# Graph attention setup: one product of 80 condition columns for neighbours and condition rows, weights loaded by chunk, and one self product moved in the loop

## The chip, the cores and the metric

The kernel runs on one core of a Trainium2 chip. The metric is the device time of one launch in microseconds (us); lower is better. A core has a matrix engine (TensorE, PE in the profile, with PEld for its weight loads), a vector engine (VectorE, DVE), a scalar engine (ScalarE, ACT), a general one (GpSimd, POOL), and SyncE (SP), which here only issues loads and stores (DMAs). ACT issues some loads too. The engines run side by side, each through its own list of instructions in order, and wait for one another on semaphores.

## The reference

Two blocks follow each other: a graph attention block over x (4 batches of 1024 rows of 512), and a transformer block modulated by a condition (4 rows of 512). All is float32. The part that the change touches is the graph block:

```python
def _forward(v, q, adj, W_self, b_self, w_bias, b_bias, Wq, bq, Wk, bk, Wout, bout):
    row_zero = v.sum(-1) == 0
    q_exp = jnp.where(row_zero[..., None], 0.0, q[:, None, :])
    vcq = jnp.concatenate([v, q_exp], axis=-1)
    self_feat = vcq @ W_self.T + b_self
    output = self_feat
    for d in range(2):
        A = adj_f if d == 0 else jnp.swapaxes(adj_f, 1, 2)
        A = A[:, :, :20, :]
        cond, vb = A.sum(-1), A @ w_bias + b_bias
        output = output + _gat_attention(self_feat, cond, vb, Wq[d], bq[d], Wk[d], bk[d], Wout[d], bout[d])
    return v + relu(output)

def _gat_attention(self_feat, cond_adj, label_bias, Wq, bq, Wk, bk, Wout, bout):
    kv = self_feat[:, :20]                       # the first 20 rows of a batch are the neighbours
    qh = (self_feat @ Wq.T + bq)                 # 16 heads of 32
    kh = (kv @ Wk.T + bk)
    aff = einsum('bnhd,bmhd->bnhm', qh, kh) / sqrt(32)
    aff = where(cond_adj[:, :, None, :] > 0, aff, -9e15) + label_bias[:, :, None, :]
    w = softmax(aff, axis=-1)
    out_t = einsum('bnhm,bmf->bnhf', w, kv)
    return einsum('bnhf,hgf->bnhg', out_t, Wout) + bout
```

The condition q enters the self features of a row only where the row's sum is not zero. So self_feat is x @ Wx + nonzero * (q @ Wq_in) + b_self, where Wx and Wq_in are the two halves of W_self, transposed. Behind it come layer norms, attention with 16 heads of 64 and a hidden layer of 2048, all modulated by the silu of the condition times W_mod. The change touches of these only the silu.

## The kernel before

The order of every engine's instructions is that in which the program is written (a manual schedule); tiles are freed by semaphores. A load carries one of eight completion semaphores in turn, and waits until the load eight places before it in the program has landed, no matter which queue either is on.

*Setup (L186 to L389).* It prepares what the graph loop reads, for 80 neighbours (4 batches of 20).

- Loads. ACT's queue issues the 80 neighbour rows into vcq (L193, four loads, one for each batch), the four condition rows cnd (L196), and the condition spread over 20 rows for each batch into the right half of vcq (L198, four loads). SP's queue issues wx (L195) and wq_in (L201), one megabyte each, then five small loads of bias vectors into rows (L210), then six weights of one megabyte (L216: for each direction d the key, output and query weights) and the output bias (L217), then the first three tiles of x, masks and small constants.
- Warming (L240): seven products of a zero tile into the banks that the loop uses first.
- neighbours(0) (L250 to L254) transposes the 80 rows with four TensorE transposes and copies them to vcqT; through_self(0) (L256 to L267) multiplies them with wx: 16 matmuls of 128x128 weights and 80 columns. DVE meanwhile finds the rows whose sum is not zero (nz, L244 and L245) and multiplies the spread condition with it (L270). neighbours(1) and through_self(1) do the same with the spread condition and wq_in, into the same bank pf.
- Between them: silu of the condition on ACT (L274), and transposes of the condition and of its silu (L279, L280). Then the vectors are transposed (L283) and the bias is added (sfT, L286).
- The condition rows' own product with wq_in (L293: four condition columns as weights, 512 columns streamed, four matmuls) gives qrows; it is stored and read back spread over 128 partitions as qrB (L298 to L300).
- keys(d) (L307), values(d) (L331), and folded(d) (L366) make keys, values and folded query weights from sfT; ACT and DVE take turns to evacuate. Between them g_sum and g_start of tiles 0 and 1 stand in ACT's and DVE's lists.

*The graph loop (L861 and on)* runs over 32 tiles of 128 rows, with its stages spread over steps s. What belongs here, by helper and line:

- g_start(i) (L182, L183, DVE): the nonzero flag of each row, then flag times qrB plus b_self, written straight into the bank pf. g_self(i) (L666, PE) adds x @ wx on it, in four matmuls of 512 columns; g_selfout (L674, ACT) copies it to sf; g_selfT (L679, PE and L681, ACT) transposes it.
- g_mask1(i) (L686, L688, POOL) makes floats of the mask (af) and multiplies them by the label weights (ab); af and ab have one buffer each. g_mask2(i) (L695 to L699, DVE) sums both to a factor and a term for each neighbour.
- g_scores (L706, PE), g_soft1 (L719, DVE), g_soft2 (L729, POOL), g_soft3 (L736, L737, DVE: maximum and subtraction), g_soft4 (L740, ACT: exp), g_soft5 (L745, L746, DVE: sum and reciprocal; L748, POOL: weights), g_weightsT (L755, PE; L756, ACT), g_startattend (L761, ACT), g_attend (L767, PE), g_rows (L779, DVE). g_startscores (L662, ACT) presets the bank of the scores.

The order of one step s before the change is:

```python
            do(g_scores, s)
            do(g_weightsT, s - 1)
            do(g_soft1, s)
            do(g_startscores, s + 1)
            do(g_startattend, s - 1)
            do(g_soft2, s)
            do(g_mask2, s + 2)
            do(g_mask1, s + 3)
            do(g_soft3, s)
            do(g_self, s + 2)
            do(g_selfT, s + 1)
            do(g_soft4, s)
            do(g_soft5, s)
            do(g_attend, s - 1)
```

and then g_selfout(s + 2), g_rows(s - 1), g_start(s + 3), g_sum(s + 4). The bank pa of the scores, the tile t of the softmax and the tile wts exist once each, so the softmax of one tile ends before that of the next begins.

Of the kernel before, what the change touches and what calls it, by code (L numbers as in the profile page):

```python
# [26 lines left out]
GH, GD, NG, NL = 16, 32, 20, 11  # L27
# [14 lines left out]
def cond_block_kernel(  # L42
# [27 lines left out]
    nc = tc.nc  # L70
    B = cond.shape[0]
    NTA = B * NT
    KV = B * NG
# [5 lines left out]
    def evac(k, o, i):  # L79

        if k % 2 == 0:
            nc.scalar.copy(o, i)
        else:
            nc.vector.tensor_copy(o, i)
# [4 lines left out]
    ident = cst.tile([P, P], F32, name="ident")  # L89
# [6 lines left out]
    V_SELF, V_K, V_Q, V_1, V_MOD = 0, FC, 3 * FC, 5 * FC, 5 * FC + MC  # L96
    vecs = cst.tile([P, N_VEC], F32, name="vecs")
# [34 lines left out]
    with ExitStack() as gctx:  # L132
# [8 lines left out]
        wx = gp.tile([P, FC, F], F32, name="wx")  # L141
        scT = gp.tile([P, FC, 32], F32, name="scT")
# [22 lines left out]
        nzs, pfs, pas, pos = {}, {}, {}, {}  # L165
# [19 lines left out]
        with ExitStack() as sctx:  # L185
            sp = sctx.enter_context(tc.tile_pool(name="sp", bufs=1))  # L186
            sps = sctx.enter_context(tc.tile_pool(name="sps", bufs=3, space=PSUM))


            vcq = sp.tile([KV, 2 * F], F32, name="vcq")  # L190
            cnd = sp.tile([B, F], F32, name="cnd")
            for b in range(B):
                nc.scalar.dma_start(vcq[b * NG : (b + 1) * NG, :F], x[b * S : b * S + NG, :])  # L193
            wq_in = sp.tile([P, FC, F], F32, name="wq_in")
            nc.sync.dma_start(wx, w_selfT[:F].rearrange("(c p) f -> p c f", p=P))  # L195
            nc.scalar.dma_start(cnd, cond)  # L196
            for b in range(B):
                nc.scalar.dma_start(  # L198
                    vcq[b * NG : (b + 1) * NG, F:], cond[b : b + 1, :].broadcast_to([NG, F])
                )  # L200
            nc.sync.dma_start(wq_in, w_selfT[F:].rearrange("(c p) f -> p c f", p=P))  # L201
            rows = sp.tile([N_VEC, P], F32, name="rows")
            for at, v in (
                (V_SELF, b_self.rearrange("(c p) -> c p", p=P)),
                (V_K, gbk.rearrange("d (c p) -> (d c) p", p=P)),
                (V_Q, gbq.rearrange("d (c p) -> (d c) p", p=P)),
                (V_1, b1.rearrange("(c p) -> c p", p=P)),
                (V_MOD, b_mod.rearrange("(c p) -> c p", p=P)),
            ):
                nc.sync.dma_start(rows[at : at + v.shape[0], :], v)  # L210
# [25 lines left out]
            for i in range(2):  # L236
                pfs[i] = bank_of("pf", i)
            pas[0], pos[0] = bank_of("pa", 0), bank_of("po", 0)
            for t in (pfs[0], pfs[1], pas[0][:, 0, :], pas[0][:, 1, :], pos[0], pos[0], pos[0]):
                nc.tensor.matmul(t, lhsT=warm[:, :P], rhs=warm, start=True, stop=True)  # L240


            nz = sp.tile([KV, 1], F32, name="nz")
            nc.vector.tensor_reduce(nz, vcq[:, :F], axis=AX.X, op=ALU.add)  # L244
            nc.vector.tensor_scalar(nz, nz, 0.0, None, ALU.not_equal)  # L245
            vcqT = sp.tile([P, 2 * FC, KV], F32, name="vcqT")
            pf = sps.tile([P, FC, KV], F32, name="pf", tag="s")

            def neighbours(h):
                pt = sps.tile([P, FC, P], F32, name="pt", tag="s")  # L250
                for c in range(FC):
                    k = h * FC + c
                    nc.tensor.transpose(pt[:, c, :KV], vcq[:, k * P : (k + 1) * P], ident[:KV, :KV])
                evac(h, vcqT[:, h * FC : (h + 1) * FC, :], pt[:, :, :KV])  # L254

            def through_self(h):  # L256
                w = (wx, wq_in)[h]
                for c in range(FC):
                    for k in range(FC):
                        nc.tensor.matmul(  # L260
                            pf[:, c, :],
                            lhsT=w[:, k, c * P : (c + 1) * P],
                            rhs=vcqT[:, h * FC + k, :],
                            start=(h == 0 and c == 0 and k == 0),
                            stop=(h == 1 and k == FC - 1),
                            skip_group_check=True,
                        )  # L267

            neighbours(0)
            nc.vector.tensor_scalar(vcq[:, F:], vcq[:, F:], nz, None, ALU.mult)  # L270
            through_self(0)
            neighbours(1)
            silu = sp.tile([B, F], F32, name="silu")
            nc.scalar.activation(silu, cnd, AF.Silu)  # L274
            condT = sp.tile([P, FC, B], F32, name="condT")
            for t, src in ((condT, cnd), (scT[:, :, :B], silu)):
                pc = sps.tile([P, FC, B], F32, name="pc", tag="s")
                for c in range(FC):
                    nc.tensor.transpose(pc[:, c, :], src[:, c * P : (c + 1) * P], ident[:B, :B])  # L279
                nc.vector.tensor_copy(t, pc)  # L280
            through_self(1)
            pv = sps.tile([P, F], F32, name="pv", tag="s")
            nc.tensor.transpose(pv[:, :N_VEC], rows, ident[:N_VEC, :N_VEC])  # L283
            nc.vector.tensor_copy(vecs, pv[:, :N_VEC])
            sfT = sp.tile([P, FC, KV], F32, name="sfT")
            nc.vector.tensor_tensor(  # L286
                sfT, pf, vecs[:, V_SELF : V_SELF + FC].unsqueeze(2).to_broadcast([P, FC, KV]), ALU.add
            )


            pq = sps.tile([P, F], F32, name="pq", tag="s")
            for c in range(FC):
                nc.tensor.matmul(  # L293
                    pq[:B], lhsT=condT[:, c, :], rhs=wq_in[:, c, :], start=(c == 0), stop=(c == FC - 1)
                )
            qrows = sp.tile([B, F], F32, name="qrows")
            nc.scalar.copy(qrows, pq[:B])
            nc.sync.dma_start(qrd, qrows)  # L298
            for b in range(B):
                nc.sync.dma_start(qrB[:, b, :], qrd[b : b + 1, :].broadcast_to([P, F]))  # L300
# [543 lines left out]
        def do(f, i):  # L844
            if 0 <= i < NTA:
                f(i)
# [14 lines left out]
        for s in range(-4, NTA + 2):  # L861
            do(g_load, s + 4)
            if s >= -2:
                do(g_loadmask, s + 4)
            if s in (1, 7, 13, 23):
                g_modload(s // 6)
            do(g_scores, s)
            if s == NTA:
                ahead(4)
            do(g_weightsT, s - 1)  # L870
            do(g_soft1, s)
            do(g_startscores, s + 1)
# [51 lines left out]
    with ExitStack() as actx:  # L924
# [298 lines left out]
        for b in range(B):  # L1223
# [22 lines left out]
            for gp in range(NP):  # L1246
                g, p = divmod(gp, 2)
                at = s0 + gp * NT
# [80 lines left out]
        for i in range(4):  # L1329
            at = NS - (10, 9, 6, 3)[i]  # L1330
# [149 lines left out]
        for s in range(NS + 1):  # L1480
# [4 lines left out]
            if s < NS:  # L1485
                b, r = divmod(s, NP * NT)
                gp, t = divmod(r, NT)
# [218 lines left out]
```

## Time and profile before

| | us |
|---|---|
| median of 3 runs | 3044.85 |
| lowest and highest | 3044.52, 3045.57 |
| the profiled execution | 3043.88 |
| its span, first to last instruction | 3041.9 |

The span falls into stretches like this (busy time of an engine in each):

| stretch, us | what runs | PE | DVE | ACT | POOL |
|---|---|---|---|---|---|
| 0 to 22.9 | setup up to keys(0) | 20.58 | 3.46 | 3.62 | 5.06 |
| 22.9 to 59.4 | keys, values, folded weights | 36.30 | 14.41 | 11.95 | 1.59 |
| 59.4 to 100 | first steps of the graph loop | 36.66 | 22.92 | 14.00 | 15.58 |
| 100 to 405 | rest of the graph loop | 300.27 | 251.55 | 129.37 | 129.73 |
| 405 to 3041 | attention, output, hidden layer | 2610.37 | 1704.51 | 1272.01 | 1186.35 |

How to read the lines of the profile: the timeline gives start, length, engine, line of the code, operation, what is written from what, shapes and count, and in brackets the idle time of the engine just before and what ended it. The chain of waits is followed back from the last instruction of a window, and gives start, length and what, in order of time. SPq and ACTq are the issue of loads by these engines. A float32 matmul stands in the trace as two instructions of TensorE; a transpose as one. A busy time of PE counts pipelined matmuls and is not a measure of full use.

### The profile page before, as it was taken

The numbers are of one execution on the slowest core, as the hardware profiler recorded it, in microseconds if no ns is written. First come the engines' busy times: TensorE is split into PE (matmuls) and PEld (weight loads), VectorE is DVE, ScalarE is ACT, GpSimd is POOL, SyncE is SP. The second block draws the span as 40 slices with busy tenths as digits, with TensorE's granted clock in tenths as the row PEclk, the third lists the DMA queues.
The fourth block names the chain that finished last, engine by engine and source line by source line (L and its number), as shares of the span: only waits on it lengthen the run. The fifth ranks groups of instructions, "written<-read, shape, count | busy, mean of one in ns | idle before, by whom it ended". The sixth has DMA issues, their size and how long they took to land.

```text
span 3041.9 us, 41802 instructions
## 1 busy us (share of the span) xinstructions
PE 3004.2 (99%) x15327; PEld 1977.4 (65%) x15327; DVE 1996.9 (66%) x2833; ACT 1430.9 (47%) x2367; POOL 1338.3 (44%) x922
## 2 busy tenths in 40 slices
PE   9999999999999999999999999999999999999999
PEld 5666655555555555555555555555568888888888
DVE  3788867787878887878877878877863222222322
ACT  2444456555755555755555755555641221122211
POOL 1444456555655655656655656655721110111010
PEclk9999999999999999999999999999999999999999
DMA  6433447777868767868767867776871010101110
GB/s 195 133 124 107 139 111 189 167 160 177 196 156 207 190 158 173 199 160 204 189 162 166 204 164 197 189 168 152 213 190 69 14 49 28 49 18 38 35 42 15
DMA packets 282719, 418.06 MB, mean 137 GB/s; under 512 B 28912, under 2 KB 101036, under 8 KB 282516
## 3 DMA queue, kind: packets, MB, share of 16 engines
q1 hardware_dynamic: 282268, 415.06, 53.6%
q8 instruction: 123, 2.02, 0.3%
q14 instruction: 80, 0.66, 0.1%
q10 hardware_dynamic: 248, 0.34, 0.0%
HBM read 121.09 MB, written 25.76 MB: 48 GB/s over the span
## 4 chain that ended last, share of the span: by engine, by line
PE 81%; DVE 7%; ACT 4%; issue 3%; POOL 2%; DMA 2%; SPq 1%; POOLq 0%; DVEq 0%; ACTq 0%
PE q L520 18%; PE psc L1139 14%; PE pav L1047 13%; PE mbd L520 5%; PE pu L1122 5%; PE mbu L520 5%; PE mad L520 4%; PE mau L520 3%; ACT w L1156 2%; PE mcd L520 2%; PE mdd L520 2%; DVE mx L1150 2%; PE mdu L520 2%; PE mcu L520 2%; POOL t L729 1%
## 5 line engine op out<-in xcount | busy, mean ns | idle before, releaser
L1165 POOL TENSOR_SCALAR w<-w,sm 128x1024 f32<-128x1024 f32 x256 | 727.8, 2843 | 704.4 <-DVE sm L1161 700.2
L1156 ACT ACTIVATE w<-psc,mx 128x1024 f32<-128x1024 f32 x512 | 570.1, 1114 | 642.1 <-DVE mx L1150 641.0
L1174 DVE STREAM_TRANSPOSE wd<-w 128x1024 f32<-128x1024 f32 x512 | 632.0, 1235 | 109.0 <-ACT w L1163 97.5
L1150 DVE TENSOR_REDUCE mx<-psc 128x1 f32<-128x1024 f32 x512 | 599.0, 1210 | 80.4 <-PE psc L1139 77.2
L1139 PE MATMUL psc<-kT,qT 64*128 64x512 f32 x2048 | 528.2, 615 | 3.8 <-ACT w L1156 1.5
L1047 PE MATMUL pav<-wT,v 128*64 128x256 f32 x4096 | 480.0, 383 | 1.8 <-DMA wT<-wd 1.8
L1047 PEld LDWEIGHTS pav<-wT,v 128*64 128x64 f32 x4096 | 292.0, 137 | 226.7 <-issue 84.5
L1139 PEld LDWEIGHTS psc<-kT,qT 64*128 64x128 f32 x2048 | 200.7, 186 | 223.3 <-issue 151.3
L1163 ACT ACTIVATE w<-w,sm 128x1024 f32<-128x1024 f32 x256 | 291.0, 1137 | 0.0
L499 POOL TENSOR_TENSOR tx<-hT 128x512 f32<-128x512 f32 x8 | 10.3, 1288 | 596.7 <-ACT hT L435 596.7
L1131 DVE TENSOR_TENSOR xr<-pu,xr 128x512 f32<-128x512 f32 x210 | 143.4, 683 | 79.5 <-PE pu L1122 79.3
L520 PE MATMUL q<-hT,wqk 128*128 128x512 f32 (+1 forms) x396 | 181.2, 581 | 1.0 <-DVE q L534 1.0
L542 ACT COPY mbu<-mau 128x512 f32<-128x512 f32 x30 | 17.1, 570 | 276.6 <-PE mau L520 276.6
L706 PE MATMUL pa<-kp,sfT 128*128 128x320 f32 x512 | 143.5, 433 | 1.5 <-ACT sfT L681 1.5
L520 PEld LDWEIGHTS q<-hT,wqk 128*128 128x128 f32 x396 | 74.7, 190 | 80.9 <-issue 78.3
L520 PE MATMUL q<-tx,ex 128*128 128x512 f32 (+1 forms) x264 | 123.5, 591 | 1.4 <-ACT hT L435 1.4
L706 PEld LDWEIGHTS pa<-kp,sfT 128*128 128x128 f32 x512 | 94.8, 190 | 38.2 <-ACT sfT L681 1.9
L666 PE MATMUL pf<-wx,xT 128*128 128x512 f32 x256 | 117.0, 601 | 0.0
L520 PE MATMUL mad<-w,hs 128*128 128x256 f32 x512 | 113.1, 379 | 0.0
L520 PEld LDWEIGHTS mad<-w,hs 128*128 128x128 f32 x512 | 97.3, 190 | 13.2
L1122 PE MATMUL pu<-wout,oT 128*128 128x256 f32 x360 | 98.4, 396 | 4.2 <-DVE sm L1161 2.2
L1122 PEld LDWEIGHTS pu<-wout,oT 128*128 128x128 f32 x360 | 62.6, 189 | 59.2 <-issue 31.6
(303 smaller groups left out, 4592.8 us busy)
## 6 DMA issues: line engine op xcount, KB each, us to landing
wT<-wd SPq DMA_DIRECT2D x1024, 256.0 KB
wqk<-in_w_qkv SPq DMA_DIRECT2D x64, 256.0 KB
xT<-in_xt SPq DMA_DIRECT2D x32, 256.0 KB
xs<-in_x SPq DMA_DIRECT2D x32, 256.0 KB
x1d<-xs SPq DMA_DIRECT2D x32, 256.0 KB
xl<-x1d SPq DMA_DIRECT2D x32, 256.0 KB
wv<-in_w_qkv SPq DMA_DIRECT2D x32, 256.0 KB
xr<-x1d SPq DMA_DIRECT2D x32, 256.0 KB
```

Of the source, the lines that this page charges most:

```text
L520: nc.tensor.matmul(t[:, q * width : (q + 1) * width], lhsT=lhs(which, q, k), rhs=rhs(which, q, k), start=(fresh and q == 0 and k == 0), st ...
L666: nc.tensor.matmul(pfs[i], lhsT=xT[i][:, c, :], rhs=wx[:, c, :], start=False, stop=(c == FC - 1), skip_group_check=True,)
L706: nc.tensor.matmul(pas[i][:, n, :HF], lhsT=sfT2[i][:, c, :], rhs=kp[:, b, c, n * HF : (n + 1) * HF], start=False, stop=(c == FC - 1), skip ...
L1047: nc.tensor.matmul(po[j * D : (j + 1) * D, :], lhsT=vt[b, g][:, m, p * P + j * D : p * P + (j + 1) * D], rhs=w[:, j, :, m, :], start=(m == 0),
L1122: nc.tensor.matmul(pu[0][:, q * HB : (q + 1) * HB], lhsT=a[:, q * P : (q + 1) * P], rhs=r, start=(bool(fresh) and q == 0), stop=True, skip ...
L1131: nc.vector.tensor_tensor(o, pu[0].rearrange("p (r f) -> p r f", r=2), o, ALU.add)
L1139: nc.tensor.matmul(sc[j][:, n * F : (n + 1) * F], lhsT=qT[b, gp][q, t * P : (t + 1) * P], rhs=kT[b, gp][q, n * F : (n + 1) * F], start=Tru ...
L1150: nc.vector.tensor_reduce(mx, sc, axis=AX.X, op=ALU.max, negate=True)
L1156: nc.scalar.activation(w, sc, AF.Exp, bias=mx, accum_out=sm)
L1163: nc.scalar.mul(w, w, sm)
L1165: nc.gpsimd.tensor_scalar(w, w, sm, None, ALU.mult)
L1174: nc.vector.transpose(wd[j][:, :, at, :], wn.pop((b, gp, t, j)).rearrange("p (m k) -> p m k", k=U))
```

## The change

- wq_in and wx are loaded in four chunks of 128 rows each, wq_in first. The spread condition is no longer loaded (vcq is half as wide). cnd is issued first on ACT's queue, and the five loads of rows move from SP's queue to ACT's, behind the neighbours.
- The warming does five products and not seven.
- The condition is transposed first (condT), spread on DVE to 80 columns (condB), and multiplied with wq_in once (pq). The result is copied to cq. Its first column for each batch (qT_) gives the condition rows, by four transposes (pr) instead of the product of 512 columns.
- The flag nz is brought into columns by a small product with the identity (pn, nzB), and multiplies cq after the product, on DVE. The bias is then added, and last the neighbours' product with wx (pf).
- through_self runs over the chunks k outside and over the output blocks c inside.
- The silu of the condition and its transposes come after the neighbours' product.
- In the loop, g_self(3) stands in step 1 directly behind the scores, ahead of the transposes of the weights. In step 0, g_start(3) and g_mask2(2) change places.

```diff
-            vcq = sp.tile([KV, 2 * F], F32, name="vcq")
+            vcq = sp.tile([KV, F], F32, name="vcq")
             cnd = sp.tile([B, F], F32, name="cnd")
-            for b in range(B):
-                nc.scalar.dma_start(vcq[b * NG : (b + 1) * NG, :F], x[b * S : b * S + NG, :])
             wq_in = sp.tile([P, FC, F], F32, name="wq_in")
-            nc.sync.dma_start(wx, w_selfT[:F].rearrange("(c p) f -> p c f", p=P))
             nc.scalar.dma_start(cnd, cond)
             for b in range(B):
-                nc.scalar.dma_start(
-                    vcq[b * NG : (b + 1) * NG, F:], cond[b : b + 1, :].broadcast_to([NG, F])
-                )
-            nc.sync.dma_start(wq_in, w_selfT[F:].rearrange("(c p) f -> p c f", p=P))
+                nc.scalar.dma_start(vcq[b * NG : (b + 1) * NG, :], x[b * S : b * S + NG, :])
+            for t, at in ((wq_in, F), (wx, 0)):
+                for k in range(FC):
+                    nc.sync.dma_start(t[:, k, :], w_selfT[at + k * P : at + (k + 1) * P])
...
-                nc.sync.dma_start(rows[at : at + v.shape[0], :], v)
+                nc.scalar.dma_start(rows[at : at + v.shape[0], :], v)
...
-            for t in (pfs[0], pfs[1], pas[0][:, 0, :], pas[0][:, 1, :], pos[0], pos[0], pos[0]):
+            for t in (pfs[0], pfs[1], pas[0][:, 0, :], pas[0][:, 1, :], pos[0]):
                 nc.tensor.matmul(t, lhsT=warm[:, :P], rhs=warm, start=True, stop=True)
...
+            def through_self(t, w, rhs):
+
+                for k in range(FC):
+                    for c in range(FC):
                         nc.tensor.matmul(
-                            pf[:, c, :],
+                            t[:, c, :],
                             lhsT=w[:, k, c * P : (c + 1) * P],
-                            rhs=vcqT[:, h * FC + k, :],
+                            rhs=rhs[:, k, :],
...
+            condT = sp.tile([P, FC, B], F32, name="condT")
+            conditionT(condT, cnd)
+            pt = sps.tile([P, FC, P], F32, name="pt", tag="s")
+            for c in range(FC):
+                nc.tensor.transpose(pt[:, c, :KV], vcq[:, c * P : (c + 1) * P], ident[:KV, :KV])
+            vcqT = sp.tile([P, FC, KV], F32, name="vcqT")
+            nc.scalar.copy(vcqT, pt[:, :, :KV])
+            condB = sp.tile([P, FC, B, NG], F32, name="condB")
+            nc.vector.tensor_copy(condB, condT.unsqueeze(3).to_broadcast([P, FC, B, NG]))
+            nz = sp.tile([KV, 1], F32, name="nz")
+            nc.vector.tensor_reduce(nz, vcq, axis=AX.X, op=ALU.add)
+            nc.vector.tensor_scalar(nz, nz, 0.0, None, ALU.not_equal)
+            pq = sps.tile([P, FC, B, NG], F32, name="pq", tag="s")
+            through_self(pq.rearrange("p c b m -> p c (b m)"), wq_in, condB.rearrange("p c b m -> p c (b m)"))
+            cq = sp.tile([P, FC, B, NG], F32, name="cq")
+            nc.scalar.copy(cq, pq)
+            pn = sps.tile([P, KV], F32, name="pn", tag="s")
+            nc.tensor.matmul(pn, lhsT=nz.to_broadcast([KV, P]), rhs=ident[:KV, :KV], start=True, stop=True)
             pv = sps.tile([P, F], F32, name="pv", tag="s")
             nc.tensor.transpose(pv[:, :N_VEC], rows, ident[:N_VEC, :N_VEC])
+            nzB = sp.tile([P, KV], F32, name="nzB")
+            nc.vector.tensor_copy(nzB, pn)
             nc.vector.tensor_copy(vecs, pv[:, :N_VEC])
+            pf = sps.tile([P, FC, KV], F32, name="pf", tag="s")
+            through_self(pf, wx, vcqT)
+            qT_ = sp.tile([P, FC, B], F32, name="qT_")
+            nc.vector.tensor_copy(qT_, cq[:, :, :, 0])
+            nc.vector.tensor_tensor(
+                cq,
+                cq,
+                nzB.rearrange("p (b m) -> p b m", b=B).unsqueeze(1).to_broadcast([P, FC, B, NG]),
+                ALU.mult,
+            )
             sfT = sp.tile([P, FC, KV], F32, name="sfT")
             nc.vector.tensor_tensor(
-                sfT, pf, vecs[:, V_SELF : V_SELF + FC].unsqueeze(2).to_broadcast([P, FC, KV]), ALU.add
+                sfT,
+                cq.rearrange("p c b m -> p c (b m)"),
+                vecs[:, V_SELF : V_SELF + FC].unsqueeze(2).to_broadcast([P, FC, KV]),
+                ALU.add,
             )
-            pq = sps.tile([P, F], F32, name="pq", tag="s")
+            nc.vector.tensor_tensor(sfT, pf, sfT, ALU.add)
+            silu = sp.tile([B, F], F32, name="silu")
+            nc.scalar.activation(silu, cnd, AF.Silu)
+            conditionT(scT[:, :, :B], silu)
+            pr = sps.tile([P, F], F32, name="pr", tag="s")
             for c in range(FC):
-                nc.tensor.matmul(
-                    pq[:B], lhsT=condT[:, c, :], rhs=wq_in[:, c, :], start=(c == 0), stop=(c == FC - 1)
-                )
+                nc.tensor.transpose(pr[:B, c * P : (c + 1) * P], qT_[:, c, :], ident)
             qrows = sp.tile([B, F], F32, name="qrows")
-            nc.scalar.copy(qrows, pq[:B])
+            nc.scalar.copy(qrows, pr[:B])
...
             do(g_scores, s)
+            if s == 1:
+
+                do(g_self, s + 2)
...
-            do(g_mask2, s + 2)
+            do(g_start if s == 0 else g_mask2, s + (3 if s == 0 else 2))
             do(g_mask1, s + 3)
             do(g_soft3, s)
-            do(g_self, s + 2)
+            if s != 1:
+                do(g_self, s + 2)
...
             if s + 3 >= 2:
-                do(g_start, s + 3)
+                do(g_mask2 if s == 0 else g_start, s + (2 if s == 0 else 3))
```

conditionT(t, src) holds the four transposes and the DVE copy that stood in a loop before. The banks of the setup come from a pool of three, in turn: pc, pt, pq, pn, pv, pf, pc, pr.

More of the change, by code (lines that the diff above doesn't have):

```diff
@@ L238, in cond_block_kernel, with conditionT @@
             pas[0], pos[0] = bank_of("pa", 0), bank_of("po", 0)
-            for t in (pfs[0], pfs[1], pas[0][:, 0, :], pas[0][:, 1, :], pos[0], pos[0], pos[0]):
+            for t in (pfs[0], pfs[1], pas[0][:, 0, :], pas[0][:, 1, :], pos[0]):
                 nc.tensor.matmul(t, lhsT=warm[:, :P], rhs=warm, start=True, stop=True)
[L243 to L259, printed above, removed]
+            def through_self(t, w, rhs):
+                for k in range(FC):
+                    for c in range(FC):
                         nc.tensor.matmul(
-                            pf[:, c, :],
+                            t[:, c, :],
                             lhsT=w[:, k, c * P : (c + 1) * P],
-                            rhs=vcqT[:, h * FC + k, :],
-                            start=(h == 0 and c == 0 and k == 0),
-                            stop=(h == 1 and k == FC - 1),
+                            rhs=rhs[:, k, :],
+                            start=(c == 0 and k == 0),
+                            stop=(k == FC - 1),
                             skip_group_check=True,
                         )
[L269 to L276, printed above, removed]
+            def conditionT(t, src):
                 pc = sps.tile([P, FC, B], F32, name="pc", tag="s")
@@ L280, in cond_block_kernel @@
                 nc.vector.tensor_copy(t, pc)
-            through_self(1)
+            condT = sp.tile([P, FC, B], F32, name="condT")
[6 more added lines that the diff above has]
+            condB = sp.tile([P, FC, B, NG], F32, name="condB")
```

## The prediction

> **What bounds the kernel now.** I read the summary of the page first, then the stretches by stage, the chain of waits of the first 30 us, and the timeline of the setup and of the first loop steps, each with its idle times.
>
> ```profile
> span 3041.9 us, 41802 instructions
> PE 3004.2 (99%) x15327; PEld 1977.4 (65%) x15327; DVE 1996.9 (66%) x2833; ACT 1430.9 (47%) x2367; POOL 1338.3 (44%) x922
> ```
>
> TensorE is busy in 99% of the span, and everything behind the graph loop comes in the same order with and without the change. So a gain exists only where TensorE starts its later work earlier: in the setup, and at the loop's first hole. The chain of waits of the setup (start, length, what):
>
> ```profile
> 5.25 1.80 PE pa L240 x4
> 7.04 2.58 PE po L240 x6
> 9.62 0.29 PE pt L253 x4
> ...
> 9.94 0.43 ACT vcqT L82
> ...
> 10.41 3.80 PE pf L260 x32
> ...
> 15.16 0.38 PE pc L279 x4
> 15.54 3.73 PE pf L260 x32
> 19.27 0.20 PE pv L283
> 19.47 3.53 PE pq L293 x8
> 23.00 3.73 PE pk L307 x32
> ```
>
> Up to 23.00, where keys(0) begins, the chain is TensorE with two short hand-offs. Loads do not stand in it, but they are near:
>
> ```profile
> 8.43 0.68 DVE L244 TENSOR_REDUCE nz<-vcq 80x1 f32<-80x512 f32 x1 [6.88 <-DMA vcq<-in_x]
> 10.43 0.27 SPq L210 DMA_DIRECT2D rows<-in_gbq  x1
> 11.54 0.40 SPq L216 DMA_DIRECT2D w<-in_gwkT  x1
> ```
>
> The neighbour rows, issued up to 2.74, are in at 8.43. SP's row loads wait one by one: in the built program each load waits for the load eight places earlier, over both queues. The third one, at 10.43, waits for wq_in, so the six attention weights are not issued before 11.54.
>
> The hole in the loop (timeline, then two stretches of 2 us, whose last three columns are granted clock, DMA share and GB/s):
>
> ```profile
> 76.63 0.81 DVE L736 TENSOR_REDUCE mx<-t 128x32 f32<-128x640 f32 x1
> 83.92 1.33 PE L755 MATMUL pt<-ident,wts 128*128 128x128 f32 x5 [2.49 <-POOL wts L748]
> 85.05 4.67 PE L666 MATMUL pf<-wx,xT 128*128 128x512 f32 x8
> 93.34 1.36 DVE L183 SCALAR_TENSOR_TENSOR pf<-qrB,nz,bsB 128x512 f32<-128x512 f32 x1
> 84.00:86.00 2.00, 2.00 (x7) 1.48 (x8) 1.25 (x2) 0.71 (x2) 1.19 (x1) 0.50 0.89 264
> 88.00:90.00 2.00, 2.00 (x10) 0.99 (x9) 1.82 (x3) 0.00 (x0) 0.21 (x1) 1.00 0.02 5
> ```
>
> TensorE ends scores(1) at 81.43 and waits 2.49 us for POOL's weights of tile 0. Then the clock is halved for a while: the self product, 3.60 us for the same eight halves at 95.96, takes 4.67.
>
> **The setup, step by step** (us of the span; each f32 matmul stands as two instructions).
> *Warming.* Ten halves instead of 14: 1.47 + 3.78 + 1.80 + 2 of the six in 2.58 (0.86) = 7.9.
> *Condition rows.* Four transposes 0.29 (as pt) give 8.2; the copy on DVE with hand-offs about 0.2. The spread copy to 80 columns (condB) is not in the trace: 0.32 by the 32x320 copies out of SBUF (L84, two in 0.65), 0.49 by the 128x320 copies. I take 0.49, the same shape: 8.93. The neighbours' four transposes (0.44) fit beside it if their rows land by 8.43 as now.
> *Condition product*, 32 halves of 80 columns: 3.80, to 12.73. Its weights are loaded first now, and the first megabyte was in by 6.4 (ACT's third broadcast at 6.41 waits for wx). The chunk waits therefore cost nothing.
> *Evacuation.* The next product needs the copy cq, which frees its operand and its bank: as 9.91 to 10.41, 0.5, to 13.24. The new nz product and the vector transpose (0.20 each, by pv) lie beside it. nz's sum and compare on DVE (0.68 + 0.15) end before 10.
> *Neighbour product*: 3.80, to 17.03. Its vcqT copy follows ACT's five row loads (0.3 each) and one table load (1.28): ready near 10. Silu follows cq with a second table load: 13.2 + 1.28 + 0.63 = 15.1. Without this product as cover they would cost up to 1.9.
> *Before keys(0)*: silu's transposes 0.38, then four for the condition rows, unseen: between 0.38 (pc, four columns) and 0.60 (the loop's 128x128 four at 66.36, the same moving width); I take 0.60. The last DVE add (0.49) ends at 17.6 beside them. The extra DVE work before it (vecs, qT_, two passes of 0.49) ends by 14.7.
> keys(0) begins at 18.0 instead of 23.0: **-5.0**, at most -5.3. In it lie 3.53 for the dropped 512-column product and 1.72 for the dropped warming, against the new transposes and the wait for condB.
>
> *Moved loads.* SP loses five row issues and gains six chunk issues; ACT loses four broadcasts and gains five rows. The first weight is then issued after wx3, which waits for the last neighbour rows: about 8, some 3 us earlier. The thin place is keys(1), needed at 18.0 + 3.73 + 3.44 = 25.2: SP's load at 27.75 waits for that weight today. With 3 us it lands near 24.5 and costs nothing; unmoved, it would cost 2.6. The first broadcast of the condition rows product, due on DVE at 49.23 - 5, is issued at 39.89 today and needs no luck.
>
> **The loop, in the times of before.** g_start(3) goes ahead of the maximum of tile 0, and g_mask2(2) behind its reciprocal.
> *DVE.* After soft1(0) (ends 73.17), g_start(3) runs while POOL adds until 74.79. At 93.34 the same instruction beside a POOL multiply (92.88 to 94.15) took 1.36 and ended 0.55 behind it; alone it takes 0.76. Hence 75.34, and the maximum begins at 75.36, not 76.63: 1.27 earlier; the reciprocal ends at 80.66.
> *POOL.* mask1(3) reuses the buffers that mask2(2) reads, so it now waits for that late mask2(2), and the weights of tile 0 are queued behind it. Sums to 81.8, cast and multiply (0.55 + 1.07) to 83.0, weights 1.27 to 1.77: 84.3 (taking 1.27, as at 92.88; the 1.77 had g_start beside it). That is 0.4 later than today.
> *PE.* The self product fills 81.43 to 84.87, and the weights are there. By the pitches of later steps (0.82 to the ACT copy, 0.59 and 0.63 to the next two, 0.59 for the last, 1.12 for attend), scores(2) begins at 88.7 instead of 91.1. That is not all kept: the next softmax starts at 84.3, not 83.9. Its exp, though, no longer stands behind the sfT copy (90.25 to 90.83), so it runs at 90.3 instead of 90.73, and soft1(2) begins at 94.3 instead of 95.69. Steps 2 and 3 wait 0.3 for the POOL weights today (105.26, 115.18): the softmax chain paces them, so **-1.4** is what lasts. Bounds: -2.4 without the slowdown beside POOL, -0.9 with the 1.77.
>
> Sum: -5.0 - 1.4 = **-6.4**. The profiled execution took 3043.88 (1.98 around its span), 0.97 under the median; from 3043.88 the sum is 3037.5, and on the median 3044.85 it is **3038.4**. Its own range is 3037.2 (-7.7) to 3038.9 (-5.9).
>
> **Rivals.**
> *The clock halves again.* From 84.87 to 87.54 TensorE would only transpose and wait for the ACT copies: 2.7 us, after 3.4 of matmuls. In before, 2.49 of waiting halved it, and the eight halves and the transposes lost 1.07 + 0.62 = 1.7. Against it, the wait proper is 1.6 of the 2.7. scores(2) would end at 94.9, soft1(2) with it: -0.75 instead of -1.4, and the time 3039.1. [...]
> *Small loads starve.* The last neighbour rows are now issued only after cnd has landed, and their transposes stand ahead of the condition product. If each took 5.7, as the last one today (2.74 to 8.43), cnd lands at 6.7 and the rows at 12.5; the product starts at 12.9, 4.0 later, and the gain is 2.4: 3042.5. A weight list that does not move gives 2.6 less: 3041.0. Against it: the second broadcast at 3.5 waits for the first small load, which was in by then.
> *Slower.* The same chain (cnd, last rows, wx3, all six weights on SP behind it) is one serial line where two free queues stood. Each us beyond 8.9 at which the rows land costs one; from 15.3 on the change loses, from 21.4 it loses 0.2%. At 22 it takes 3051.5. Nothing in the trace shows a small load over 6 us.
>
> **From these to the numbers.** 0.2% is 6.1 us, about what a measurement here can tell from no change; the forecast lies just beyond it. Forecast 0.73, of which 0.09 ends within 0.2%; clock 0.13; starved loads 0.09, both within; slower 0.05. Faster 0.64, same 0.31, slower 0.05. The range takes in the clock rival, an unmoved weight list and the better bounds: 3036.9 to 3041.2.
>
> **What would show it.** Right: keys(0) near 18.0, the rows landed before 8.5, no wait of keys(1); scores(1), self product, transposes without a hole, POOL weights ending some 9 us behind the start of the maximum, clock 1.00 there, and soft1(2) 6.4 before its old 95.69. Wrong: a load as releaser of the neighbours' transposes, of pv or of pk; a stretch of clock 0.5 near 81 to 85; or a later stage that waits for its own loads and gives the shift back.

## The result, and the profile after

| | before | after |
|---|---|---|
| median, us | 3044.98 (10 runs, 3044.09 to 3047.70) | 3038.26 (10 runs, 3035.60 to 3042.74) |
| ratio after to before | | 0.9976, interval 0.9968 to 0.9984 |
| the profiled execution, its span | 3043.88, 3041.9 | 3036.06, 3034.2 |

The change makes the kernel 0.24% faster, between 0.16% and 0.32%. The medians differ by 6.7 us.

The head of the page after:

```profile
span 3034.2 us, 41780 instructions
PE 2999.3 (99%) x15317; PEld 1980.2 (65%) x15317; DVE 1999.6 (66%) x2836; ACT 1432.0 (47%) x2368; POOL 1339.4 (44%) x922
```

TensorE still fills 99%, with 4.9 us less busy time. The chain of waits of the setup after (start, length, what):

```profile
5.25 2.06 PE pa L237 x4
7.31 0.86 PE po L237 x2
8.17 0.35 PE pc L255 x4
...
8.55 0.19 DVE condT L256
...
8.76 0.34 DVE condB L268
...
9.14 3.81 PE pq L243 x32
...
12.97 0.43 ACT cq L275
...
13.45 3.80 PE pf L243 x32
17.25 0.34 PE pc L255 x4
17.59 0.53 PE pr L308 x4
18.11 3.53 PE pk L320 x32
```

From the condition's transposes (pc at 8.17) to keys(0) (pk, 18.11) every piece is the one that the forecast listed. No load stands in the chain. Here the chain prints the start of keys(0) 0.16 later than the timeline does (17.95), where before they were 0.07 apart (23.00 and 22.93); the table below uses the timeline for all.

The loop's first steps after, on TensorE (timeline: start, length, engine, line, what, count, idle time before and what ended it), then on DVE and POOL:

```profile
72.32 4.57 PE L719 MATMUL pa<-kp,sfT 128*128 128x320 f32 x16 [0.73 <-ACT sfT L694]
76.73 3.60 PE L679 MATMUL pf<-wx,xT 128*128 128x512 f32 x8
80.17 0.71 PE L768 MATMUL pt<-ident,wts 128*128 128x128 f32 x5
80.71 0.60 PE L692 MATMUL pt<-ident,sf 128*128 128x128 f32 x4
82.77 1.38 PE L780 MATMUL po<-vb,wT 128*128 128x128 f32 x10 [1.46 <-ACT po L774]
83.99 4.47 PE L719 MATMUL pa<-kp,sfT 128*128 128x320 f32 x16
```

```profile
68.73 2.08 DVE L183 SCALAR_TENSOR_TENSOR pf<-qrB,nz,bsB 128x512 f32<-128x512 f32 x1
70.73 0.81 DVE L749 TENSOR_REDUCE mx<-t 128x32 f32<-128x640 f32 x1
75.65 0.55 DVE L708 TENSOR_REDUCE on<-af 128x40 f32<-128x440 f32 x1
89.27 0.81 DVE L732 TENSOR_TENSOR t<-pa,mul 128x640 f32<-128x640 f32 x1
```

```profile
76.33 0.55 POOL L699 CAST af<-a 128x440 f32<-128x440 int32 x1 [6.07 <-DVE on L708]
76.96 1.08 POOL L701 TENSOR_TENSOR ab<-af,wb 128x440 f32<-128x440 f32 x1
78.01 1.27 POOL L761 TENSOR_TENSOR wts<-t,sm 128x640 f32<-128x640 f32 x1
```

The self product (76.73) fills the old hole, the weights of tile 0 are there at 79.28, and a hole of 1.46 us appears behind the transposes instead of 2.49 ahead of them. Nowhere between 76 and 90 us is the clock halved. soft1(2) begins at 89.27, 6.42 us before its old 95.69.

The first 100 us of all profiles, cut at the same instructions. soft1(0) follows the first self product by 12.85 or 12.86 in every one of them. "Clock" is the time from which it is granted in full, counted like all times from the first instruction of the same profile.

| kernel | clock | keys(0) | to keys(1) | to self product 0 | soft1(0) to soft1(2) | soft1(2) at |
|---|---|---|---|---|---|---|
| before | 5.28 | 22.93 | 7.07 | 29.50 | 23.34 | 95.69 |
| before, second run | 7.32 | 23.94 | 7.07 | 29.50 | 23.45 | 96.82 |
| before, third run | 6.96 | 23.77 | 7.07 | 29.50 | 23.45 | 96.64 |
| after | 5.82 | 17.95 | 6.97 | 30.04 | 21.46 | 89.27 |
| after, second run | 5.80 | 17.94 | 8.00 | 30.11 | 21.44 | 90.34 |
| setup part alone | 6.89 | 18.48 | 6.97 | 30.04 | 21.45 | 89.80 |
| loop part alone | 7.22 | 23.89 | 7.07 | 29.50 | 21.74 | 95.06 |
| after, no exchange | 6.72 | 18.40 | 6.97 | 30.04 | 22.11 | 90.37 |
| after, mask1(3) late | 5.73 | 17.90 | 6.97 | 30.04 | 20.89 | 88.65 |
| after, rows on SP | 7.22 | 18.65 | 6.97 | 29.50 | 21.43 | 89.40 |
| after, one load each | 5.67 | 17.90 | 6.97 | 30.04 | 21.74 | 89.50 |
| after, rows product | 7.09 | 21.67 | 7.07 | 29.50 | 21.44 | 92.54 |
| before, warming 5 | 7.66 | 22.40 | 7.07 | 30.04 | 21.76 | 94.12 |
| setup alone, warming 7 | 6.21 | 19.86 | 6.97 | 30.04 | 23.14 | 92.87 |

Three things are read from it. The shift of 6.42 is made of -4.98 (keys(0)), -0.10, +0.54 (a loss between keys(1) and the loop) and -1.88 (the loop's first steps). The last column but one falls into two groups, 23.1 to 23.5 and 20.9 to 22.1: the first holds only kernels with the old order of the loop, the second holds both orders. And keys(0) moves with the clock, half a microsecond for each one by which the release comes later: keys(0) less half the release is 20.28 to 20.29 in the four profiles with the setup of before, and 15.03 to 15.07 in the seven with the setup of the change. So at an equal release the setup is worth 5.2 us; 4.98 is what the profiled pair shows, because the change had its release 0.54 later.

From soft1(2) to the last soft1 (near 400 us) all 14 profiles need 304.7 to 305.1, and from there to the end 2639.9 to 2645.9, without regard to the change: 2641.3, 2644.4 and 2641.4 before, 2640.1 and 2642.0 after. So the 7.7 us between the two profiled spans are 6.5 of the change and 1.2 of that scatter.

### The profile page after: what moved, and what is told of

Read it like the earlier page. It is cut to its first block, busy times and chain, and to the rows that moved or that the text cites. A ratio compares the mean times of both kernels' runs of the same rounds, so it can differ in the third digit from the quotient of the medians.

```text
span 3034.2 us, 41780 instructions
## 1 busy us (share of the span) xinstructions
PE 2999.3 (99%) x15317; PEld 1980.2 (65%) x15317; DVE 1999.6 (66%) x2836; ACT 1432.0 (47%) x2368; POOL 1339.4 (44%) x922
## 4 chain that ended last, share of the span: by engine, by line
PE 83%; DVE 7%; ACT 3%; POOL 3%; issue 2%; DMA 2%; SPq 1%; POOLq 0%; DVEq 0%; ACTq 0%
PE q L533 19%; PE psc L1156 15%; PE pav L1064 13%; PE pu L1139 6%; PE mbd L533 5%; PE mbu L533 5%; PE mad L533 4%; PE mau L533 3%; PE mcd L533 2%; PE mdd L533 2%; PE mdu L533 2%; PE mcu L533 2%; DVE mx L1167 1%; ACT w L1173 1%; POOL t L742 1%
```

## The experiments

**The two parts alone.** Setup part alone: the kernel after, with the loop's old order.

```diff
-            if s == 1:
-                do(g_self, s + 2)
-            do(g_start if s == 0 else g_mask2, s + (3 if s == 0 else 2))
+            do(g_mask2, s + 2)
```

and the other two loop lines back likewise. Loop part alone: the kernel before with these loop lines of the change.

> The setup of the changed kernel with the loop of before. By the forecast the two parts add: keys(0) begins near 18.1 as in the changed kernel, the loop keeps its hole of 2.5 us with the halved clock, the third soft1 (step 2, 95.69 in before, 89.27 in the changed kernel) begins near 90.8, and the time is 5.0 under before. Rival 1: the hole depends on where it falls; 5 us earlier the clock is not halved and the third soft1 comes near 90.0. Rival 2: the loads of the loop (SP's list moves by 3, TensorE by 5) come late, so that the loop starts with new waits and the third soft1 is at 91.5 or later.

> The loop of the changed kernel with the setup of before. Forecast: keys(0) stays at 23.0, no hole behind scores(1), clock 1.00 there, the third soft1 at 94.3 (1.4 earlier), time 1.4 under before. Rival: the clock is halved behind the transposes and the third soft1 comes at 94.9. Other bounds: 93.3 if the softmax chain is not slowed beside POOL, 94.8 with the longer POOL multiply.

Setup alone: median 3038.92 (11 runs), ratio 0.9979 [0.9970, 0.9988]. Loop alone: 3043.51 (11 runs), 0.9996 [0.9987, 1.0005]; the kernel before beside them 3045.40 (31 runs). The setup alone has the whole gain that can be measured. Its TensorE in the loop (timeline, then two stretches of 3.41 us; columns: busy time of PE, PEld, DVE, ACT, POOL, then granted clock, DMA share, GB/s):

```profile
79.62 0.76 PE L768 MATMUL pt<-ident,wts 128*128 128x128 f32 x5 [2.20 <-POOL wts L761]
80.23 3.60 PE L679 MATMUL pf<-wx,xT 128*128 128x512 f32 x8
```

```profile
75.16:78.57 3.41, 2.26 (x9) 1.28 (x7) 1.94 (x4) 2.32 (x5) 0.79 (x1) 1.00 0.88 283
78.57:81.98 3.41, 2.35 (x10) 1.40 (x11) 1.34 (x2) 1.55 (x3) 2.47 (x2) 1.00 0.86 250
```

The old order and its hole (2.20) are still there, but the self product takes 3.60, not 4.67: the clock is not halved. From soft1(0) to soft1(2) it needs 21.45, as the whole change does (21.46). The loop part alone does remove the hole and gets 21.74. (Its soft1(2) is at 95.06 and not at the expected 94.3, because its release came at 7.22 and keys(0) at 23.89; behind keys(0) it is 71.17, where 71.4 was expected.) So both parts remove the same 1.6 to 1.9 us, and together they remove it once. What the two kernels have in common is that the clock stays full. The mean granted clock of every run on record points the same way, though it does not tell where in the span a clock was halved: of the 31 runs of the kernel before 29 show 0.999 or less; of the 11 runs of each part alone 2 do, and of the 10 of the change none.

**When the clock halves.** In the profile before, the clock is full from 5.28 and halved from 83.79 to 87.20. In the clock record of that trace the halved stretch is 3.413 us long and begins 78.507 us behind the release, 23.0 times its own length. From these two numbers comes the author's estimate of a grid: steps of 3.413 us, counted from the release. Whether a step is halved would then depend on how busy TensorE was in the step ahead; that is a theory, and the runs below try it. Two more runs of the kernel before, unchanged:

> The kernel before, unchanged, in another execution. The setup alone gave a loop without a halved clock although its hole stayed, and a third soft1 71.3 behind keys(0), as early as with the loop's change. If the halving depends on where the hole falls against the clock's windows, counted from its release near 5.5, the third soft1 comes 72.8 behind keys(0) with a halved clock and 71.3 to 71.6 without it; the change in the loop is then worth 1.4 only in the executions of the first kind. If instead the hole itself costs what the forecast says, it comes 72.8 behind keys(0) either way.

> The same once more, as for b2: the third soft1 72.8 behind keys(0) with a halved clock at the hole and 71.3 to 71.6 without, or 72.8 either way.

Releases at 7.32 and 6.96, halved from 85.83 and 85.47: 78.51 behind the release in all three. soft1(0) to soft1(2) 23.45 both. The two runs took 3048.18 and 3044.98. Then the hole was moved on the grid: in the kernel before by less warming alone, in the setup part by the old warming.

```diff
-            for t in (pfs[0], pfs[1], pas[0][:, 0, :], pas[0][:, 1, :], pos[0], pos[0], pos[0]):
+            for t in (pfs[0], pfs[1], pas[0][:, 0, :], pas[0][:, 1, :], pos[0]):
```

(and the reverse). The first of the two expectations below counts from releases at 5.5, 7.0 and 7.2 in the kernel before; the traces have 5.28, 6.96 and 7.32.

> The kernel before with ten warming halves instead of 14 and nothing else. The warming term: keys(0) begins 1.72 earlier than in the kernel before, counted from the release of the clock (before: 17.4 behind it with a release at 5.5, 16.8 with releases at 7.0 and 7.2), so near 15.0 to 15.7 behind it. The hole ahead of the transposed weights of tile 0 stays 2.5 us long but moves 1.72 against the 3.413 us steps in which the clock is granted, counted from the release. Theory A, the clock halves only where one whole step is almost empty: the idle time is shared by two steps (0.9 to 1.6 us in each), the clock stays full, and the third soft1 comes 71.2 to 71.5 behind keys(0) instead of 72.8. Theory B, a wait of 2.4 us or more halves it wherever it lies: halved for 3.4 us behind the hole as in three profiles of the kernel before, and 72.8 behind keys(0).

> The setup part alone with the old 14 warming halves: keys(0) 1.72 later than in the setup part alone (18.5 with a release at 6.9), near 20.2 with such a release. The hole of 2.2 us moves by 1.72 into the middle of one step of 3.413 us. Theory A (one step almost empty): 1.2 of 3.4 us of the step are then busy, between the 0.9 that halved the clock and the 2.3 that did not; I lean to halved, and the third soft1 comes 72.5 to 72.9 behind keys(0). Theory B (the length of the wait, 2.4 or more): not halved, 71.3.

The steps of the grid around the hole: third run of the kernel before, before with warming 5, setup with warming 7 (columns as above).

```profile
82.06:85.47 3.41, 0.91 (x7) 0.70 (x7) 2.17 (x5) 0.57 (x2) 1.77 (x1) 1.00 0.81 259
85.47:88.88 3.41, 3.41 (x6) 1.35 (x5) 2.20 (x6) 1.81 (x3) 2.93 (x3) 0.50 0.70 212
```

```profile
79.34:82.76 3.42, 2.10 (x8) 1.14 (x6) 1.93 (x4) 2.46 (x5) 0.63 (x1) 1.00 0.94 301
82.76:86.17 3.41, 2.22 (x9) 1.37 (x10) 1.36 (x3) 1.42 (x3) 2.47 (x2) 1.00 0.87 275
```

```profile
77.89:81.30 3.41, 1.20 (x7) 0.62 (x6) 2.17 (x5) 0.98 (x3) 1.80 (x1) 1.00 0.84 260
81.30:84.72 3.42, 3.42 (x9) 1.87 (x8) 2.21 (x6) 1.81 (x3) 2.53 (x3) 0.50 0.79 253
```

The transposes behind the hole and the self product, in before with warming 5, then in setup with warming 7 (timeline):

```profile
83.95 0.77 PE L755 MATMUL pt<-ident,wts 128*128 128x128 f32 x5 [2.50 <-POOL wts L748]
84.55 3.60 PE L666 MATMUL pf<-wx,xT 128*128 128x512 f32 x8
```

```profile
81.01 1.09 PE L768 MATMUL pt<-ident,wts 128*128 128x128 f32 x5 [2.21 <-POOL wts L761]
81.90 5.00 PE L679 MATMUL pf<-wx,xT 128*128 128x512 f32 x8
```

Less warming leaves the hole at 2.50 us, but it is shared by two steps (2.10 and 2.22 us busy), and the clock stays full: 21.76 instead of 23.45 in the second and third run. More warming leaves the hole of the setup part at 2.21, puts it into one step (1.20 busy), and the next step is halved, from 75.09 behind the release, which is 22 steps of 3.413: 23.14 instead of 21.45. So the length of the wait alone does not decide: behind a wait of 2.50 the clock stayed full, behind one of 2.21 it was halved. What goes with the halved clock is how empty one step was. From 66 to 108 us in ten of the profiles, and in the three or four steps around the hole in the other four, a halved step came behind each step with 0.90 to 1.20 us of TensorE's busy time, and behind none with 1.95 or more. The price is 1.69 us in both pairs. Theory A held, theory B fell; behind keys(0) soft1(2) came at 71.72 and 73.01, 0.1 to 0.2 beyond what was expected. keys(0) with warming 5 came 14.7 behind the release and not 15.0 to 15.7, since the release at 7.66 was later than any that was counted from.

**The exchange in step 0, and POOL's queue.** After with the old places of g_start and g_mask2; and after with mask1(3) put behind the weights of tile 0 in POOL's list.

```diff
-            do(g_start if s == 0 else g_mask2, s + (3 if s == 0 else 2))
+            do(g_mask2, s + 2)
...
-                do(g_mask2 if s == 0 else g_start, s + (2 if s == 0 else 3))
+                do(g_start, s + 3)
```

```diff
-            do(g_mask1, s + 3)
+            if s != 0:
+                do(g_mask1, s + 3)
...
             do(g_soft5, s)
+            if s == 0:
+                do(g_mask1, s + 3)
```

> The changed kernel without the exchange of g_start(3) and g_mask2(2) in step 0; the self product still stands directly behind the scores. By the rows of before g_start(3) ends only at 82.75 (77.8 in the time of this kernel), so the self product waits some 1.3 us, the weights of tile 0 come at their old distance, scores(2) ends 1.4 later, and the third soft1 begins near 89.7 instead of 89.27: the exchange is worth 0.4 to 0.5. Rival: it is worth the whole 1.3 that the maximum gained, third soft1 near 90.5. Rival: it costs, because mask1(3) no longer waits for the late mask2(2); third soft1 before 89.2.

> The changed kernel with g_mask1(3) in step 0 behind g_soft5(0), so that the weights of tile 0 do not queue on POOL behind mask1(3), which waits for the late mask2(2). If that queue is what the exchange gave back, the weights end near 77.2 instead of 79.28, the second soft1 begins near 78.1 (DVE is then busy with mask2(2)), and the third soft1 is bound by scores(2), which starts at 84.0 as now: near 88.6, 0.7 earlier. Rival: the weights were covered anyway by the self product, TensorE sets the pace and the third soft1 stays at 89.2.

No exchange: 3038.04 (11 runs), ratio 0.9976 [0.9967, 0.9985]. mask1(3) late: 3039.09 (9 runs), 0.9980 [0.9970, 0.9990]. In time neither differs from the change; in the trace both do. Without the exchange the self product waits for its preset (first line below), and soft1(2) comes 0.65 later behind soft1(0); 0.4 to 0.5 was expected. With mask1(3) late POOL's weights end 2.2 us earlier (second line, start 75.83 against 78.01), of which 0.57 arrives at soft1(2), where 0.7 was expected: the softmax of the next tile paces the rest. No version was measurably better than the change.

```profile
78.43 3.70 PE L679 MATMUL pf<-wx,xT 128*128 128x512 f32 x8 [1.08 <-DVE pf L183]
```

```profile
75.83 1.27 POOL L761 TENSOR_TENSOR wts<-t,sm 128x640 f32<-128x640 f32 x1 [5.62 <-DVE sm L759]
```

**The loads.** After with the five rows loads back on SP; after with one load of a megabyte for each of wq_in and wx.

```diff
-                nc.scalar.dma_start(rows[at : at + v.shape[0], :], v)
+                nc.sync.dma_start(rows[at : at + v.shape[0], :], v)
```

```diff
-                for k in range(FC):
-                    nc.sync.dma_start(t[:, k, :], w_selfT[at + k * P : at + (k + 1) * P])
+                nc.sync.dma_start(t, w_selfT[at : at + F].rearrange("(c p) f -> p c f", p=P))
```

> The changed kernel with the five loads of bias vectors back on SP's queue, behind the chunks. keys(0) stays near 18.0. SP issues the first attention weight near 9.2 instead of 7.71, so the key weight of direction 1 lands 1.5 later, near 25.7 instead of 24.2, and keys(1), which is due at 25, waits 0.5 to 1.0 for it. Rival: the weights are limited by what the DMA engines move, and land as before, keys(1) without a wait. Rival: the vectors land too late for their transpose behind the condition product, and keys(0) itself is late.

> The changed kernel with wq_in and wx in one load each instead of four chunks. By the forecast the chunk waits cost and gain nothing: the first megabyte is in before the condition product starts at 9.1, so keys(0) begins within 0.3 of 18.0. Rival: with both megabytes queued at once the neighbour rows land near 8.4 again instead of 7.3, their transposes hold the product back, and keys(0) begins 0.3 to 1.0 later.

Rows on SP (one run, 3040.14): they are issued between 5.71 and 7.49 without the waits of before, the first weight at 8.16 instead of 7.71, and keys(1) does not wait (6.97). One load each (one run, 3036.28): keys(0) at 17.90 with a release at 5.67, against 17.95 with one at 5.82. So neither the chunks nor the other queue for the rows carry the gain.

**Two terms of the sum, and the change once more.** After with the product of 512 columns back in place of the four transposes:

```diff
-                nc.tensor.transpose(pr[:B, c * P : (c + 1) * P], qT_[:, c, :], ident)
+                nc.tensor.matmul(
+                    pr[:B], lhsT=condT[:, c, :], rhs=wq_in[:, c, :], start=(c == 0), stop=(c == FC - 1)
+                )
```

> The kernel after with the 512-column product of the condition rows put back in place of its four transposes. Forecast's terms: 3.53 for the product against 0.60, so keys(0) begins 2.9 to 3.0 later, near 21.0 (20.9 to 21.6 with the release of the clock). Rival: the product lies beside the last two adds and costs less than 2.

> The kernel after once more. By theory A nothing between 76 and 90 us halves the clock (the busiest wait lies between products): third soft1 71.2 to 71.5 behind keys(0). If the one profile was luck, the clock is halved near 82 and it is 72 or more. The gain or loss of a further 1.4 us behind 800 us that other profiles show is not of the change: it may come or not.

The chain of waits of the first:

```profile
17.88 0.34 PE pc L255 x4
18.21 3.53 PE pr L308 x8
21.74 3.73 PE pk L322 x32
```

3.53 for the product where the change has 0.53: 3.0 us, on the chain and in full; keys(0) is at 21.67, 3.0 behind the 18.65 of the kernel with nearly the same release (rows on SP), and 0.1 behind the latest time expected. One run, 3041.20. The warming term (1.72) is seen in the two kernels above. Less half the release, keys(0) is at 16.76 in the setup part with seven warming products and at 15.04 with five, and in the kernel before at 20.29 and 18.57: 1.72 both times.

The second run of the change (3038.87) has soft1(2) 72.40 behind keys(0), which was to mean a halved clock. It does not: the clock is full from 5.80 to the end of the kernel's work, and the loop's part is 21.44. What is longer is the way to keys(1), the thin place that the forecast named; a load that releases pk was one of its signs of being wrong (timeline):

```profile
25.82 0.33 SPq L155 DMA_DIRECT2D xT<-in_xt  x1
25.94 3.77 PE L320 MATMUL pk<-sfT,w 128*128 128x80 f32 x32 [0.86 <-DMA w<-in_gwkT]
```

keys(1) waits for its weight here and begins 1.03 later behind keys(0) than in the first run. SP's load of x, which is issued once that weight has landed, tells the landing: 25.82 here, 24.21 in the first run, 23.34 to 24.42 in the five others with keys(0) before 19. The stretch from 12 to 16 us suggests why it comes no earlier, which no run tests (after, then before; DMA share and GB/s are last):

```profile
12.00:16.00 4.00, 3.91 (x35) 3.69 (x34) 1.49 (x5) 2.34 (x3) 0.00 (x0) 1.00 0.97 351
```

```profile
12.00:16.00 4.00, 3.66 (x37) 3.50 (x36) 0.75 (x3) 0.30 (x1) 0.00 (x0) 1.00 0.86 244
```

The transfer engines are full from 12 us on after the change (0.97 to 1.06 in each stretch of 4 us up to 28), where the kernel before reached that at 16.

## Why the prediction was right, and where its steps were off

The time forecast was 3038.4, measured were 3038.26; the shift at soft1(2) was 6.4 forecast, 6.42 measured in the profiled pair. That good a match is partly luck. In the trace two terms that the forecast did not have cancel (0.54 lost ahead of the loop, 0.48 more gained in it), and so do a setup that is 0.2 better than forecast and a release that came 0.54 later in the profile after, which cost 0.27. Single runs of the change scatter from 3035.60 to 3042.74, so a median 0.1 from the forecast is luck too.

- *Setup, -5.0.* Right: 4.98 in the profiled pair, 5.2 at an equal release, with nearly every piece as listed. condB took 0.34 where 0.49 was taken, the transposes of the condition rows 0.53 where 0.60 was taken. The product of 512 columns was worth 3.0, as forecast (3.53 less 0.60), shown by putting it back. The warming is worth 1.72, as forecast.
- *Between keys(1) and the loop, nothing forecast.* 0.54 was lost there. TensorE waits at one place among the folded weights:

```profile
46.78 2.42 PE L379 MATMUL pw<-kbd,w 128*128 128x320 f32 x8 [0.52 <-ACT qbB L82]
```

In 8 of the 14 profiles this stretch takes 30.04 or 30.11, in 6 it takes 29.50. The loss is not bound to an edit: the kernel before shows it with less warming, and the change with the rows on SP does not. The instructions and their waits are the same in both kinds, so the author takes it for a matter of when they meet; what decides it was not tried and stays open.
- *Loop, -1.4.* Measured -1.88 between soft1(0) and soft1(2). The step that was mis-sized is "POOL": the forecast put mask1(3) behind both sums of the late mask2(2). The cast waits only for the first sum (L708, ending 76.20) and runs beside the second, so the weights of tile 0 ended 0.5 earlier than forecast (79.28, that is 83.82 in the times of before, against 84.3). The softmax of tile 1 starts on their end, and soft1(2) comes 0.5 earlier than forecast (93.81 in the times of before, against 94.3). scores(2) came 0.2 earlier (88.53 against 88.7), which the weights don't explain: the self product covers them until 80.33. The DVE part was right: g_start(3) ended at 70.81, 75.35 in the times of before, against 75.34.
- *Where the loop's gain comes from.* Here the reasoning fell short though the size was near. The forecast took it from the filled hole. The runs show that the halved clock behind the hole was the cost (1.7 us), and that the setup part removes this too, by moving the hole on the grid. With a full clock the new order gains next to nothing at soft1(2): 21.45 and 21.76 without it, 21.43 to 21.74 with it. What it may add is a margin: none of the eight profiles with the self product moved has the clock halved in these steps. But two of the six profiles with the old order kept it full too (setup part alone, and before with warming 5).
- *Moved loads, 0.* Half right. In the first run the weight for keys(1) landed by 24.21 (24.5 forecast) and cost nothing; in the second it cost 1.03. The price of an unmoved list, 2.6, was not tested: with the rows back on SP the first weight is issued at 8.16, still ahead of the 11.54 of before, and keys(1) does not wait.
- *Rivals.* "The clock halves again" did not come in any of the eight profiles with the self product moved: the emptiest stretch of 3.41 us there holds 1.95 to 2.64 us of TensorE's busy time. "Small loads starve" and "slower" did not come: the chain's first pieces wait for no load.

## What to carry to other kernels

Here the filled hole was by itself worth next to nothing, because the softmax paced the next stage: with a full clock soft1(0) to soft1(2) took 21.45 with the hole (setup part alone) and 21.46 without it (the change). The hole's price, 1.69 us, was the clock that was halved behind it. So before reordering, look in the profile for stretches of halved clock, and at how busy TensorE was just ahead of them: here 0.90 to 1.20 of 3.41 us, and 1.72 us of warming, taken out or put in, removed the loss in one kernel and created it in another. And when a chain in front is shortened, look at the transfers that it ran beside: after this change the weights for keys(1) come with full transfer engines (a share of 0.97 to 1.06), between 1.0 us late and 2.1 early, so the next cut in the setup will find them first.

## What the runs showed of the hardware that was not expected

- The release of the clock at the start lay between 5.28 and 7.66 us in 14 profiles. In before the weight loads of the warming begin 0.85 to 0.86 us apart ahead of it (2.48, 3.33, 4.19, 5.04) and 0.43 apart behind it (5.59, 6.02, 6.45, 6.88), so keys(0) of the kernel before was at 22.93, 23.77 and 23.94 with releases at 5.28, 6.96 and 7.32: one of the sources of the scatter between runs.
- The stage behind 400 us differs by up to 6 us between executions (2639.9 to 2645.9). In two of the profiles (mask1(3) late, rows on SP) the clock was halved for 3.4 to 6.8 us near 810, in a stage that none of the edits touches. The steps of the grid ahead of it held 2.08 and 1.42 us of TensorE's busy time, part of it with weights of 64 rows (64x128, from 806.27 and 809.19 on). With mask1(3) late it was halved for two steps (the step ahead, then these two):

```profile
804.45:807.86 3.41, 2.08 (x7) 0.68 (x7) 1.61 (x4) 3.41 (x6) 0.16 (x1) 1.00 0.86 258
807.86:811.28 3.42, 3.42 (x10) 1.14 (x8) 3.23 (x4) 2.41 (x4) 2.68 (x1) 0.50 0.72 108
811.28:814.69 3.41, 3.41 (x17) 1.70 (x14) 2.12 (x4) 3.28 (x6) 1.09 (x1) 0.50 0.86 228
```

A halved step came behind 2.08 there, and behind 1.95 in the graph loop it did not. The first halved step was busy throughout (3.42) and the next was halved still, while in the graph loop, in setup with warming 7, the stretch behind a halved step that was busy throughout (3.42) had the full clock (1.00 from 84.90 to 88.32). So busy time as the trace counts it is not just what decides; which work counts as how busy stays open.
